# Windowed attention and a gated low-rank layer on one core: the first ten and last eight slots written out as sequences, a new order between them, key/value buffers for each tile

## The chip, the core and the metric

The kernel runs on one core of a Trainium2 chip. A core has five engines with a queue of instructions each: TensorE (PE, matrix products; its weight loads, PEld, run beside them), VectorE (DVE), ScalarE (ACT), GpSimd (POOL) and SyncE (SP, which here only starts DMA transfers). Each engine takes its own instructions in order; between engines there are only semaphores. Products land in PSUM, a small memory in banks of 512 fp32 values for each of 128 partitions; everything else lies in SBUF. The metric is the device time of one execution in microseconds (us), the median of several runs.

## The reference

For each of 32 sequences of 512 tokens with 256 features, all in fp32:

```python
x = x + attn(layernorm(x))     # 16 query heads, 4 key/value heads, head size 64
x = x + ffn(layernorm(x))

# attn: q, k, v = x @ wq.T, x @ wk.T, x @ wv.T;  q, k = rmsnorm(q), rmsnorm(k)
mask = (i >= j) & (i - j < 128)
scores = where(mask, q @ k.T / sqrt(64), -inf)
y = softmax(scores) @ v        # then y @ wo.T

# ffn: gate = softmax(x @ gate_w.T)            (8 experts)
#      out  = x @ weight.T + (1/16) * sum over e of gate[e] * lora_V[e] @ (lora_U[e] @ x)
```

## The kernel before

**Tiles.** A tile is 128 tokens, four to a sequence, 128 in all; `i` counts the tiles and `t = i % 4` is the place in the sequence. A query sees 128 keys, so a tile needs its own keys and values and those of the tile before; at `t == 0` there is no tile before, and a few steps are shorter or fall away (`vdiff`, `pick`, the products with `other`).

**Steps of a tile.** They are methods of `Tile`:
- `ln1_stats`, `ln1_rs` (DVE, POOL): the layernorm's rows. The mean is taken out of the weights instead, by `center` (L194), once for each weight at the start.
- `xT_pe`, `xT_copy`: x is transposed on PE and copied to SBUF by ACT. `kv_pe` and `q_pe(0)`, `q_pe(1)` are the projections.
- Three instructions read the key/value bank: `ksq` (ACT, squares of k), `vdiff` (DVE, two instructions on 64 partitions each: own values minus those of the tile before) and `kv_copy` (ACT, L296). The copy goes into one part of a tile `s.kv` that a sequence shares.
- `q_copy`, `qsq` (ACT), `ksum`, `qsum` (DVE), `pow` (POOL, L214), `kn`, `qn` (POOL): the rmsnorm of q and k.
- `trk`, `trq` (DVE) transpose in blocks of 32, and `move(n)` (L236) carries the blocks across partitions with 16 DMAs from SP's queue. One move takes the probabilities of tile n and the q and k of tile n + 3 together. `kT_copy` (ACT) scales the moved k.
- `s_pe(j)`, j = 0 to 3: the scores of 32 queries; `s_merge`, `nmaxs` (DVE), `exps` (ACT, four exponentials with their sums); `prob_den` (DVE), `prob` (POOL), `tr(j)` (DVE, into the blocks of the move).
- `pick` (POOL), `y_pe`, `y_copy`, `o_pe`, `o_add`: values, output projection, residual.
- `ln2_stats`, `ln2_rs`, `hT_pe`, `hT_copy`, `f_pe`, `gmax`, `gexp`, `gmul`, `uT_pe`, `uT_copy`, `lora_pe`, `store`: the second layer and the write to memory.

**Order.** The scheduler of the framework is switched off for all five engines inside the main block: each engine executes its instructions in the order in which `slot(i)` (L605) writes them. Slot i mixes steps of eight tiles, i to i - 7, and there are 135 slots; in the first seven and last seven some of the tiles don't exist and their steps fall away. The framework adds the semaphores.

**Buffers.** PSUM is divided by a table (L102): four single banks B0 to B3 and two double ones, S0 and S1. Products of one tag share its bank, so a product waits until the last reader of the previous one is through. `BUFS` gives the number of SBUF buffers of each kind. `load_x(i + 3)` at the end of slot i starts the load of a later tile.

Of the kernel before, what the change touches and what calls it, by code (L numbers as in the profile page):

```python
# [8 lines left out]
F32 = mybir.dt.float32  # L9
I32 = mybir.dt.int32  # L10
AF = mybir.ActivationFunctionType
# [3 lines left out]
P = 128  # L15
D = 256
HD = 64
# [13 lines left out]
def tile_window_attn_lora_ffn(  # L31
# [42 lines left out]
    nc = tc.nc  # L74
    B, T, _ = x.shape
    NT = T // P
    N = B * NT
# [3 lines left out]
    KD = KV * HD  # L81
# [3 lines left out]
    AHEAD = 3  # L85
# [10 lines left out]
    seq = ctx.enter_context(tc.tile_pool(name="seq", bufs=3))  # L96
# [4 lines left out]

    BANK = {}  # L102
    for tag, products in {
        "B0": "xT y0 kv uT",
        "B1": "f",
        "B2": "y1 o hT",
        "B3": "q1 q0",
        "S0": "s2 s0",
        "S1": "s1 s3",
    }.items():  # L110
        BANK.update(dict.fromkeys(products.split(), tag))

    def bank(what, name):
        shape = [P, 2, 512] if BANK[what][0] == "S" else [P, 512]
        return psum.tile(shape, F32, tag=BANK[what], name=f"{what}_ps_{name}")
# [1 line left out]

    BUFS = {
        "ksq": 2,
        "q": 2,  # L120
        "qsq": 2,
        "kn": 2,
        "qn": 2,
# [9 lines left out]
        "other": 3,  # L133
        "tr": 2,
        "pT": 2,
    }

    def buf(what, shape, name):
        return work.tile(shape, F32, tag=what, name=f"{what}_{name}", bufs=BUFS[what])
# [5 lines left out]
    xs = {}  # L145

    def load_x(i):
        if i < N:
            b, t = divmod(i, NT)
            xs[i] = work.tile([P, D], F32, tag="x", name=f"x_{b}_{t}", bufs=XBUFS)  # L150
            nc.sync.dma_start(xs[i], x[b, t * P : (t + 1) * P, :])


    for i in range(AHEAD):
        load_x(i)
# [8 lines left out]
    wf_sb = const.tile([P, ND, UG + D], F32, name="wf_sb")  # L164
# [29 lines left out]
    def center(w, what):  # L194

        n = w.shape[-1]
        mean = bank(what, "mean")
        for c in range(ND):
            nc.tensor.matmul(mean[:, :n], mean_m, w[:, c, :], start=(c == 0), stop=(c == ND - 1))
        for c in range(ND):  # L200
            nc.vector.tensor_tensor(w[:, c, :], w[:, c, :], mean[:, :n], ALU.subtract)

    center(wkv_sb, "kv")
    for gp in range(GP):
        center(wq_sb[:, :, gp * 512 : (gp + 1) * 512], f"q{gp}")
    center(wf_sb, "f")

    minus_half = const.tile([P, NH + KV], F32, name="minus_half")
    nc.vector.memset(minus_half, -0.5)
# [26 lines left out]
    def move(n):  # L236
        if not -DELTA <= n < N:
            return
        lo = 0 if n >= 0 else QO
        hi = PIECE if n + DELTA < N else QO  # L240
        moved[n] = buf("pT", [P, NB, PIECE], str(n))
        for b in range(NB):
            for c in range(NB):
                nc.sync.dma_start(  # L244
                    moved[n][b * BL : (b + 1) * BL, c, lo:hi],
                    blocks[n][c * BL : (c + 1) * BL, b, lo:hi],
                )

    class Tile:
# [41 lines left out]
                )  # L291

        def kv_copy(self):
            if self.t == 0:
                self.s.kv = seq.tile([P, NT, 2 * KD], F32, tag="kv", name=f"kv_{self.b}", bufs=3)
            nc.scalar.activation(self.s.kv[:, self.t, :], self.ps["kv"], AF.Copy, scale=self.ln1.rs)  # L296

        def ksq(self):
            self.k_sq = buf("ksq", [P, KD], self.n)
# [35 lines left out]
        def kn(self):  # L335
            self.k_n = buf("kn", [P, KD], self.n)
            nc.gpsimd.tensor_tensor(
                self.k_n.rearrange("p (g d) -> p g d", d=HD),
                self.s.kv[:, self.t, :KD].rearrange("p (g d) -> p g d", d=HD),
                self.rs[:, NH:].unsqueeze(2).to_broadcast([P, KV, HD]),  # L340
                ALU.mult,
            )
# [121 lines left out]
        def vdiff(self):  # L464

            if self.t == 0:
                return
            self.vd = buf("vd", [P, KD], self.n)
            own, old = self.ps["kv"][:, KD:], self.s.kv[:, self.t - 1, KD:]
            lo, hi = slice(0, H), slice(H, P)  # L470
            nc.vector.scalar_tensor_tensor(  # L471
                self.vd[lo], own[lo], self.ln1.rs[lo], old[lo], ALU.mult, ALU.subtract
            )
            nc.vector.scalar_tensor_tensor(  # L474
                self.vd[hi], own[hi], self.minus_rs[hi], old[hi], ALU.mult, ALU.add
            )

        def y_pe(self):


            ps = [self.bank(f"y{e}") for e in range(2)]

            def product(gp, half, e, v, w, start, stop):
                v0 = (2 * gp + half) * HD
                nc.tensor.matmul(  # L485
                    ps[e][half * HD : (half + 1) * HD, gp * 4 * H : (gp + 1) * 4 * H],
                    v[:, v0 : v0 + HD],
                    w.rearrange("p h (c a q) -> p a h c q", c=2, a=2)[:, half],
                    start=start, stop=stop, skip_group_check=True,
                )  # L490

            for gp in range(GP):
                for e in range(2):
                    v = self.s.kv[:, max(self.t - 1 + e, 0), KD:]
                    for half in range(2):
                        product(gp, half, e, v, self.probs(gp, e), gp == 0, self.t == 0)
            if self.t > 0:
                for gp in range(GP):
                    for half, e in ((0, 0), (1, 1), (1, 0), (0, 1)):
                        rows = slice(e * H, (e + 1) * H)  # L500
                        product(gp, half, e, self.vd[rows], self.other[gp][rows], False, True)
# [92 lines left out]
    tiles = {}  # L594
# [5 lines left out]
    nothing = Nothing()  # L600

    def at(i):
        return tiles[i] if 0 <= i < N else nothing

    def slot(i):  # L605
        if 0 <= i < N:
            tiles[i] = Tile(i)
        at(i).ln1_stats()
        at(i).xT_pe()
        at(i - 7).f_pe()  # L610
        at(i - 4).tr(2)
        at(i).xT_copy()
        at(i - 1).q_copy(0)
        at(i).ln1_rs()
        at(i - 4).tr(3)
        at(i - 1).qsq(0)
        at(i - 6).y_pe()
        at(i - 3).exps(0)
        at(i - 7).ln2_rs()
        at(i - 1).qsum()  # L620
        at(i - 4).tr(0)
        at(i - 1).pow()
        at(i - 4).tr(1)
        at(i - 3).s_pe(2)
        at(i - 6).y_copy(0)
        at(i - 7).gmax()
        at(i - 3).s_pe(1)
        at(i - 6).y_copy(1)
        at(i - 3).s_merge(2)
        at(i).kv_pe()  # L630
        at(i - 7).gexp()
        at(i - 3).nmaxs(2)
        at(i - 3).s_merge(1)
        at(i - 3).nmaxs(1)
        at(i - 7).gmul()
        at(i - 6).o_pe()
        at(i).ksq()
        at(i).vdiff()
        at(i - 1).kn()
        at(i).kv_copy()  # L640
        at(i - 1).qn()
        at(i - 2).kT_copy()
        at(i).ksum()
        at(i - 3).exps(2)
        at(i - 1).trk()
        at(i - 5).pick(0)
        at(i - 3).exps(1)
        at(i - 1).trq()
        at(i - 7).uT_pe()
        at(i).q_pe(1)  # L650
        at(i - 3).prob_den(1)
        at(i - 6).o_add()
        at(i - 7).uT_copy()
        move(i - 4)
        at(i - 3).prob(1)
        at(i - 3).prob_den(0)
        at(i - 6).ln2_stats()
        at(i - 2).s_pe(3)
        at(i).q_copy(1)
        at(i - 2).s_pe(0)  # L660
        at(i).qsq(1)
        at(i - 2).s_merge(3)
        at(i - 6).hT_pe()
        at(i - 2).nmaxs(3)
        at(i - 3).prob(0)
        at(i - 7).lora_pe()
        at(i).q_pe(0)
        at(i - 6).hT_copy()
        at(i - 2).s_merge(0)
        at(i - 2).nmaxs(0)  # L670
        at(i - 2).exps(3)
        at(i - 7).store()
        at(i - 5).pick(1)
        load_x(i + AHEAD)

    with tc.manual_schedule(engines={mybir.EngineType.PE, mybir.EngineType.Activation, mybir.EngineType.DVE, mybir.EngineType.Pool, mybir.EngineType.SP}):
        for i in range(N + 7):
            slot(i)

# [1 line left out]
_INS = ["x", "wq", "wkv", "wo", "norm_w", "w_ug", "w_base", "w_v"]  # L681
# [45 lines left out]
```

## Time and profile before

| | |
|---|---|
| median of 3 runs (lowest to highest) | 2259.92 us (2259.31 to 2261.94) |
| the profiled execution | 2258.15 us |
| its span, first to last instruction | 2256.2 us |
| mean granted TensorE clock | 0.989 |
| DMA | 257.77 MB, mean 114 GB/s |
| q1 (all but the loads of constants), share of 16 engines | 46.5% |

All durations below are from the one profiled execution. A row of the table of groups has the line, the engine, the operation, the tile written and those read, then the count, the busy time in us and the mean in ns. A row of the timeline has the start in us, the length, and the same names; what stands in brackets is idle time of the engine before it and who ended it. A row of the table of waits has who waited for whom, the sum in us, how often, and the longest. Matmuls overlap, so the time that one takes is read from start to start, not from its length. Every fp32 matmul appears as two instructions.

### The profile page before, as it was taken

The numbers are of one execution on the slowest core, as the hardware profiler recorded it, in microseconds if no ns is written. First come the engines' busy times: TensorE is split into PE (matmuls) and PEld (weight loads), VectorE is DVE, ScalarE is ACT, GpSimd is POOL, SyncE is SP. The second block draws the span as 40 slices with busy tenths as digits, with TensorE's granted clock in tenths as the row PEclk, the third lists the DMA queues.
The fourth block names the chain that finished last, engine by engine and source line by source line (L and its number), as shares of the span: only waits on it lengthen the run. The fifth ranks groups of instructions, "written<-read, shape, count | busy, mean of one in ns | idle before, by whom it ended". The sixth has DMA issues, their size and how long they took to land.

```text
span 2256.2 us, 43995 instructions
## 1 busy us (share of the span) xinstructions
PE 2145.9 (95%) x12688; PEld 1340.5 (59%) x12688; DVE 1734.7 (77%) x4300; ACT 1508.3 (67%) x5889; POOL 1807.1 (80%) x1771
## 2 busy tenths in 40 slices
PE   5799999999999999999999999999999999999997
PEld 2366566666566666566666566666566666566654
DVE  3577877777877777877777877777877777877773
ACT  2567667767767767767767767767767767767762
POOL 3598788888888888888888888888888888888873
PEclk8799999999999999999999999999999999999999
DMA  2344444544544454544544544544544544544542
GB/s 93 72 111 116 119 118 114 120 118 114 120 118 114 118 120 114 123 116 114 122 117 113 123 116 114 123 116 113 123 116 114 123 116 113 123 116 114 123 112 65
DMA packets 140127, 257.77 MB, mean 114 GB/s; under 512 B 37872, under 2 KB 73840, under 8 KB 139888
## 3 DMA queue, kind: packets, MB, share of 16 engines
q1 hardware_dynamic: 137472, 251.81, 46.5%
q10 hardware_dynamic: 2416, 3.16, 0.4%
q8 instruction: 103, 1.69, 0.3%
q14 instruction: 136, 1.11, 0.2%
HBM read 19.93 MB, written 16.78 MB: 16 GB/s over the span
## 4 chain that ended last, share of the span: by engine, by line
PE 66%; ACT 17%; DVE 9%; issue 4%; SPq 2%; DMA 1%; POOL 1%; ACTq 1%; DVEq 0%; POOLq 0%
PE y_ps L485 14%; PE s_ps L387 13%; PE q_ps L305 12%; ACT ex L414 12%; PE kv_ps L289 8%; PE f_ps L543 7%; PE o_ps L512 5%; PE f_ps L581 2%; ACT kT L369 2%; DVE nmax L403 2%; PE hT_ps L530 2%; DVE vd L474 2%; DVE vd L471 2%; SPq L244 2%; PE xT_ps L277 1%
## 5 line engine op out<-in xcount | busy, mean ns | idle before, releaser
L414 ACT ACTIVATE ex<-s_ps,nmax 128x128 f32<-128x128 f32 x2048 | 722.1, 381 | 13.2 <-DVE nmax L403 11.7
L426 POOL TENSOR_TENSOR ex<-ex,rden 128x1024 f32<-128x1024 f32 x256 | 479.9, 1896 | 130.9 <-DVE rden L422 125.8
L305 PE MATMUL q_ps<-wq_sb,xT 128*128 128x512 f32 x1024 | 489.0, 600 | 3.2 <-ACT qsq L318 3.2
L512 PE MATMUL o_ps<-wo_sb,yT 128*128 128x256 f32 x2048 | 463.5, 379 | 3.7 <-ACT yT L506 3.7
L214 POOL TENSOR_TENSOR rs<-rs,minus_half 128x20 f32<-128x20 f32 x128 | 457.5, 3574 | 10.7
L512 PEld LDWEIGHTS o_ps<-wo_sb,yT 128*128 128x128 f32 x2048 | 388.6, 190 | 110.2 <-issue 58.4
L414 ACT ACTIVATION_READ_ACCUMULATOR ex<-s_ps,nmax 128x1 f32 x2048 | 454.0, 222 | 0.0
L387 PEld LDWEIGHTS s_ps<-kT,pT 64*128 64x128 f32 x4000 | 276.5, 187 | 194.6 <-ACT ex L414 135.6
L387 PE MATMUL s_ps<-kT,pT 64*128 64x160 f32 (+4 forms) x4000 | 329.7, 300 | 45.9 <-ACT ex L414 45.9
L403 DVE TENSOR_REDUCE nmax<-s_ps 128x4 f32<-128x512 f32 x512 | 353.8, 691 | 17.6
L457 POOL TENSOR_SCALAR_AFFINE_SELECT other<-pT 64x512 f32<-64x512 f32 x384 | 299.9, 781 | 22.2 <-DMA pT<-tr 9.5
L305 PEld LDWEIGHTS q_ps<-wq_sb,xT 128*128 128x128 f32 x1024 | 187.2, 193 | 150.1 <-issue 129.4
L437 DVE STREAM_TRANSPOSE tr<-ex 128x256 f32<-128x256 f32 (+3 forms) x512 | 239.7, 487 | 29.1 <-DMA pT<-tr 25.0
L289 PE MATMUL kv_ps<-wkv_sb,xT 128*128 128x512 f32 x512 | 257.8, 626 | 1.0 <-ACT xT L283 1.0
L485 PE MATMUL y_ps<-pT,kv 128*64 128x256 f32 x2048 | 250.1, 386 | 0.5 <-ACT xT L283 0.5
L506 ACT COPY yT<-y_ps 128x512 f32<-128x512 f32 x256 | 138.6, 599 | 160.6 <-PE y_ps L485 160.6
L346 POOL TENSOR_TENSOR qn<-q,rs 128x1024 f32<-128x1024 f32 x128 | 243.4, 1901 | 0.0
L398 DVE COPY_PREDICATED s_ps<-over,s_ps 128x128 f32<-128x128 int32 x512 | 149.5, 292 | 98.9 <-PE s_ps L387 94.4
L300 ACT ACTIVATE ksq<-kv_ps,ln_rs_a 128x256 f32<-128x256 f32 x128 | 60.6, 473 | 243.3 <-PE kv_ps L289 232.3
L485 PEld LDWEIGHTS y_ps<-pT,kv 128*64 128x64 f32 x2048 | 136.1, 137 | 128.0 <-ACT q L313 50.8
L543 PE MATMUL f_ps<-wf_sb,hT 128*128 128x392 f32 x512 | 193.2, 500 | 18.0 <-ACT xT L283 12.1
L313 ACT ACTIVATE q<-q_ps,ln_rs_a 128x512 f32<-128x512 f32 x256 | 182.7, 714 | 27.9 <-PE q_ps L305 27.9
(83 smaller groups left out, 2716.3 us busy)
## 6 DMA issues: line engine op xcount, KB each, us to landing
pT<-tr SPq DMA_DIRECT2D x2000, 104.0 KB, 2.2
x<-in_x_dram SPq DMA_DIRECT2D x128, 128.0 KB, 2.3
out_dram<-res SPq DMA_DIRECT2D x128, 128.0 KB, 1.9
pT<-tr SPq DMA_DIRECT2D x48, 64.0 KB, 2.0
wq_sb<-in_wq_dram ACTq DMA_DIRECT2D x1, 1024.0 KB, 7.1
wo_sb<-in_wo_dram ACTq DMA_DIRECT2D x1, 1024.0 KB, 9.3
pT_-3_205<-tr_-3_199 SPq DMA_DIRECT2D x16, 40.0 KB, 1.9
pT_-2_274<-tr_-2_268 SPq DMA_DIRECT2D x16, 40.0 KB, 1.9
```

Source lines behind the costliest of these rows:

```text
L214: nc.gpsimd.tensor_tensor(o, o, minus_half[:, :n], ALU.pow)
L289: nc.tensor.matmul(ps, self.xT[:, c, :], wkv_sb[:, c, :], start=(c == 0), stop=(c == ND - 1))
L305: nc.tensor.matmul(ps, self.xT[:, c, :], wq_sb[:, c, gp * 512 : (gp + 1) * 512], start=(c == 0), stop=(c == ND - 1),)
L346: nc.gpsimd.tensor_tensor(self.q_n.rearrange("p (g d) -> p g d", d=HD), self.q.rearrange("p g (h d) -> p (g h) d", d=HD), self.rs[:, :NH]. ...
L387: nc.tensor.matmul(ps[:, half, gp, o0:n], qT[rows, gp * P : (gp + 1) * P], self.s.kT[rows, gp, k0 + o0 : k0 + n], start=True, stop=True,)
L403: nc.vector.tensor_reduce(self.nmax[j], ps[:, :, :, :P], AX.X, ALU.max, negate=True)
L414: nc.scalar.activation(self.ex[e][:, c, gp, half], ps[:, gp, half, :P], AF.Exp, bias=self.nmax[j][:, gp, half : half + 1], accum_out=self. ...
L426: nc.gpsimd.tensor_tensor(ex, ex, self.rden[e].rearrange("p c g a -> p (c g a)").unsqueeze(2).to_broadcast([P, 8, P]), ALU.mult,)
L457: nc.gpsimd.affine_select(out=self.other[gp][rows].rearrange("p h (c a q) -> p h c a q", c=2, a=2), in_=fr.rearrange("p h (c a q) -> p h c ...
L485: nc.tensor.matmul(ps[e][half * HD : (half + 1) * HD, gp * 4 * H : (gp + 1) * 4 * H], v[:, v0 : v0 + HD], w.rearrange("p h (c a q) -> p a ...
L512: nc.tensor.matmul(ps[:, :D], self.yT[:, c].rearrange("p e t -> p (e t)"), wo_sb[:, c, :], start=(c == 0), stop=(c == NCH - 1),)
L543: nc.tensor.matmul(ps[:, : UG + D], self.hT[:, c, :], wf_sb[:, c, :], start=(c == 0), stop=(c == ND - 1),)
```

## The change

Four things are changed; no operation is added or removed, and each tile goes through the same steps.

1. The first ten slots become one list, `FIRST`, and the last eight another, `LAST`. An entry is an operation, an argument and a tile (`s_pe.2:0` is `s_pe(2)` of tile 0; in `LAST`, tiles count from the end). `in_order` calls them one by one. `slot(i)` runs for i = 10 to 127 only.
2. Within `slot` the order is new. All four `s_pe` of tile i - 3 are in slot i (before, two of them were in the slot before); `uT_copy`, `lora_pe` and `store` belong to tile i - 8 instead of i - 7, `hT_pe` to i - 7 instead of i - 6, `pick(1)` to i - 6 instead of i - 5. The products are divided anew among the PSUM banks.
3. `kv_copy` writes a buffer of its own for each tile (eight of them) instead of a part of the sequence's tile; `kn`, `vdiff` and `y_pe` read there. q has three buffers instead of two.
4. The centring of the weight `wf` moves from the start into `FIRST`, behind `q_pe.0:2`.

```diff
-        "B0": "xT y0 kv uT",
-        "B1": "f",
-        "B2": "y1 o hT",
-        "B3": "q1 q0",
-        "S0": "s2 s0",
-        "S1": "s1 s3",
+        "B0": "xT hT y0 kv",
+        "B1": "q1 uT",
+        "B2": "y1 o q0",
+        "B3": "f",
+        "S0": "s0 s2",
+        "S1": "s3 s1",
...
-        "q": 2,
+        "q": 3,
...
+        "kv": 8,
...
-        if i < N:
+        if i < N and i not in xs:
...
-    center(wf_sb, "f")
...
         def kv_copy(self):
-            if self.t == 0:
-                self.s.kv = seq.tile([P, NT, 2 * KD], F32, tag="kv", name=f"kv_{self.b}", bufs=3)
-            nc.scalar.activation(self.s.kv[:, self.t, :], self.ps["kv"], AF.Copy, scale=self.ln1.rs)
+            self.kv = buf("kv", [P, 2 * KD], self.n)
+            nc.scalar.activation(self.kv, self.ps["kv"], AF.Copy, scale=self.ln1.rs)
...
-            own, old = self.ps["kv"][:, KD:], self.s.kv[:, self.t - 1, KD:]
+            own, old = self.ps["kv"][:, KD:], tiles[self.i - 1].kv[:, KD:]
```

The order of a slot after the change, and the two lists cut to their beginnings and ends (one line of the slot holds several calls here; `-3` is tile i - 3):

```
ln1_stats:0 xT_pe:0 s_pe.0:-3 uT_copy:-8 tr.2:-4 xT_copy:0 s_pe.3:-3 ln1_rs:0 q_copy.0:-1
s_merge.0:-3 qsq.0:-1 hT_pe:-7 nmaxs.0:-3 q_pe.1:0 pick.1:-6 hT_copy:-7 qsum:-1 exps.0:-3
s_merge.3:-3 lora_pe:-8 nmaxs.3:-3 pow:-1 q_copy.1:0 y_pe:-6 tr.3:-4 qsq.1:0 tr.0:-4 exps.3:-3
tr.1:-4 store:-8 s_pe.2:-3 y_copy.0:-6 s_pe.1:-3 y_copy.1:-6 kn:-1 s_merge.2:-3 f_pe:-7 qn:-1
kT_copy:-2 trk:-1 nmaxs.2:-3 o_pe:-6 s_merge.1:-3 nmaxs.1:-3 exps.2:-3 pick.0:-5 trq:-1 exps.1:-3
prob_den.1:-3 gmax:-7 move:-4 prob.1:-3 gexp:-7 kv_pe:0 prob_den.0:-3 o_add:-6 ln2_stats:-6
prob.0:-3 gmul:-7 q_pe.0:0 ksq:0 vdiff:0 kv_copy:0 ln2_rs:-6 ksum:0 uT_pe:-7 load_x:+3
```
```diff
+    FIRST = """
+        ln1_stats:0 xT_pe:0 ln1_stats:1 xT_copy:0 ln1_rs:0 q_pe.1:0 ln1_stats:2 ln1_stats:3 ln1_rs:1
+        kv_pe:0 q_copy.1:0 ln1_rs:2 qsq.1:0 q_pe.0:0 ln1_rs:3 vdiff:0 ksq:0 kv_copy:0 ksum:0 xT_pe:1
+        q_copy.0:0 xT_copy:1 qsq.0:0 q_pe.1:1 qsum:0 kv_pe:1 pow:0 q_copy.1:1 qsq.1:1 q_pe.0:1
+        vdiff:1 ksq:1 kv_copy:1 ksum:1 xT_pe:2 q_copy.0:1 kn:0 xT_copy:2 qsq.0:1 qn:0 q_pe.1:2 trk:0
+        qsum:1 kv_pe:2 pow:1 trq:0 q_copy.1:2 qsq.1:2 move:-3 q_pe.0:2 center_f:0 vdiff:2 ksq:2
...
+        xT_pe:4 q_copy.0:3 kn:2 xT_copy:4 qsq.0:3 qn:2 q_pe.1:4 qsum:3 move:-2 kv_pe:4 ln1_rs:4
+        pow:3 trk:2 kT_copy:0 trq:2 q_copy.1:4 s_pe.0:0 qsq.1:4 s_pe.3:0 ksq:4 s_merge.0:0 kv_copy:4
...
+    LAST = """
...
+        nmaxs.3:-3 tr.3:-4 exps.3:-3 s_pe.2:-3 tr.0:-4 store:-8 y_copy.0:-6 s_merge.2:-3 kn:-1
+        s_pe.1:-3 nmaxs.2:-3 y_copy.1:-6 qn:-1 f_pe:-7 trk:-1 s_merge.1:-3 nmaxs.1:-3 kT_copy:-2
+        o_pe:-6 pick.0:-5 exps.1:-3 trq:-1 gmax:-7 pick.1:-5 move:-4 prob_den.0:-3 gexp:-7 exps.2:-3
...
+        store:-3 ln2_rs:-2 y_pe:-1 f_pe:-2 y_copy.0:-1 y_copy.1:-1 o_pe:-1 gmax:-2 gexp:-2 gmul:-2
+        uT_pe:-2 o_add:-1 uT_copy:-2 ln2_stats:-1 hT_pe:-1 lora_pe:-2 hT_copy:-1 ln2_rs:-1 store:-2
+        f_pe:-1 gmax:-1 gexp:-1 gmul:-1 uT_pe:-1 uT_copy:-1 lora_pe:-1 store:-1
+    """
+
+    def in_order(table, base):
+        for entry in table.split():
+            op, i = entry.split(":")
+            op, _, arg = op.partition(".")
+            i = base + int(i)
+            if op == "center_f":
+                center(wf_sb, "f")
+                continue
+            if op == "move":
+                move(i)
+                continue
+            if i not in tiles:
+                load_x(i + AHEAD)
+            getattr(at(i), op)(*map(int, arg))
+
     with tc.manual_schedule(engines={...}):
-        for i in range(N + 7):
+        in_order(FIRST, 0)
+        for i in range(10, N - 1 + 1):
             slot(i)
+        in_order(LAST, N)
```

## The prediction

> **What bounds the kernel now.** I read the page first (busy shares and slices), then the table of waits, then one period of TensorE (PE) in order of time, then the reads of one key/value bank, then both ends of the run.
>
> ```profile
> PE 2145.9 (95%) x12688; PEld 1340.5 (59%) x12688; DVE 1734.7 (77%) x4300; ACT 1508.3 (67%) x5889; POOL 1807.1 (80%) x1771
> PE   5799999999999999999999999999999999999997
> PEclk8799999999999999999999999999999999999999
> ```
> PE is the bound from the third slice to the last; nothing else is above 80%. The slack is in the first two slices (113 us), the last one, and in small waits between. The waits:
>
> ```profile
> ACT kv L296 <- DVE vd L474: 115.7, 96, 1.7
> PE s_ps L387 <- ACT ex L414: 61.0, 101, 3.8
> DVE vd L471 <- ACT ksq L300: 31.8, 65, 3.3
> ```
> Only the second is PE's own. The steady run repeats every four tiles (one sequence): xT starts at 1004.78 and again at 1072.47, so 67.69 us for four slots, 16.92 each. One slot of these has no wait on PE:
>
> ```profile
> 1022.78 0.38 PE L277 MATMUL xT_ps<-ident,x 128*128 128x128 f32 x2
> 1028.60 1.98 PE L289 MATMUL kv_ps<-wkv_sb,xT 128*128 128x512 f32 x4
> 1030.42 3.62 PE L512 MATMUL o_ps<-wo_sb,yT 128*128 128x256 f32 x16
> 1033.98 1.88 PE L305 MATMUL q_ps<-wq_sb,xT 128*128 128x512 f32 x4
> ...
> 1039.51 0.38 PE L277 MATMUL xT_ps<-ident,x 128*128 128x128 f32 x2
> ```
> First column start, second length. 1022.78 to 1039.51 is 16.73 us: the floor of a full slot. Start to start, that is xT 0.22, f 1.41, y 1.88+1.02, s 1.29 twice, kv 1.82, o 3.45, uT 0.11, q 1.81+1.72, hT 0.27, lora 0.43. In the other three slots q to s takes 2.63, 2.15 and 2.14 instead of 1.81 (s waits for the exponentials of its bank), and xT to f once 0.79 instead of 0.22: 0.82+0.34+0.33+0.57, and 0.07 three times for the restart, 2.27 us in 67.69. The floor of four slots is 65.42, 16.36 each.
>
> **The change, the middle (118 slots, tiles 10 to 127).** All matmuls stay. Switches between full and 64-row tiles cost about 0.1 each (q to s 1.81 against q to xT 1.72), and there are six in both orders, so the floor stays. I laid the new order out against this floor, xT at 0: s0 and s3 0.3 to 1.6, hT, q1 1.9, lora 3.6, y 4.1, s2 and s1 7.0 to 8.3, f 8.3, o 9.7, kv 13.2, q0 14.9, uT 16.6, next xT 16.73.
>
> The waits of s go. exps of s0 end near 3.8 and of s3 near 6.4 (1.36 per call, with q_copy and qsq, 0.58 each, between); s2 and s1 need their banks at 7.0 and 7.7. exps of s2 and s1 end near 10.4 and 11.8, needed at 17. With a short y (first tile of a sequence) s1 comes at 6.7 and still fits. f needs the store of the tile before (VectorE, DVE, near 6.8, needed 8.3). GpSimd (POOL) has 15.6 us of work in a full slot (pow 3.9, two prob 3.8, picks 3.2, qn and kn 2.5, the rows of two layernorms 2.2), less than a slot. SyncE's 16 move DMAs take 10.1 us; trq ends near 11.3, they land 2 us after the last, near 6 of the next slot, before kT_copy near 8. The transposes of DVE keep their order behind them. That is worth up to 2.27 per four slots, 67 us in 118 slots.
>
> What is late next is the key/value bank. It has three readers on two engines, and xT shares it (B0 in both orders):
>
> ```profile
> 1045.33 1.98 PE L289 MATMUL kv_ps<-wkv_sb,xT 128*128 128x512 f32 x4
> 1047.41 0.47 ACT L300 ACTIVATE ksq<-kv_ps,ln_rs_a 128x256 f32<-128x256 f32 x1 [1.89 <-PE kv_ps L289]
> 1047.91 0.48 DVE L471 SCALAR_TENSOR_TENSOR vd<-kv_ps,ln_rs_a,kv 64x256 f32<-64x256 f32 x1 [0.54 <-ACT ksq L300]
> 1048.40 0.49 DVE L474 SCALAR_TENSOR_TENSOR vd<-kv_ps,minus_rs,kv 64x256 f32<-64x256 f32 x1
> 1048.93 0.69 ACT L296 ACTIVATE kv<-kv_ps,ln_rs_a 128x512 f32<-128x512 f32 x1 [1.05 <-DVE vd L474]
> ```
> They read one after the other: 4.29 us from the first kv matmul to the end of the last read, 4.19 without the switch from s. Before, o (3.45), uT and q1 lie behind kv and hide it. Now only q0 (1.72) and uT (0.11) do: xT can start at 13.18 + 4.19 + 0.06 (an exponential's end to its s: 1018.94 to 1019.00) = 17.43 instead of 16.73. **A new wait of 0.70 us**, in the three slots of four that have a vdiff; without vdiff the copy ends near 16.3 and nothing waits. PE is in order, so the whole next slot queues behind this xT.
>
> Do the own buffers remove kv_copy's wait for vdiff? Read by the row alone, kv_copy could wait because it writes the tile of which vdiff reads the previous part; then the wait falls and the stall is 0. But vdiff waits for ksq with no tensor between them except the bank (it starts 0.03 after ksq ends). The Trainium skill, PSUM — Partial Sum Buffer, "PSUM bank collisions raise a hardware error", says that two engines must not be in one bank and the same 32 partitions at once, reads against reads included. By that rule own buffers change nothing: middle (65.42 + 3 x 0.70)/4 = 16.88. By the buffer reading 16.36. I take the rule: 118 x (16.92 - 16.88) = **5 us saved** (0 to 10; the 0.06 and the switch penalties are good to 0.1 us per slot, so -7 to +17). Third q buffer, eight kv buffers: no reader of a buffer is still at work when its turn comes (y of tile i-7 reads kv of i-8 a slot before it is overwritten): nothing. Loads of x come earlier in FIRST, 0.45 each on an SP that is idle until 30: nothing.
>
> **The first ten slots.** Before, slot 10 starts at 176.34. Its PE work at floor rates (ten xT, kv, q; seven s; four y and o; three f) is 102 us. Why so long:
>
> ```profile
> 26.35 3.56 POOL L214 TENSOR_TENSOR rs<-rs,minus_half 128x20 f32<-128x20 f32 x1
> 33.76 10.09 SPq L244 DMA_DIRECT2D pT_-3_205<-tr_-3_199  x16
> 45.83 1.99 PE L387 MATMUL s_ps<-kT,pT_-3_205 64*128 64x128 f32 x16 [10.36 <-ACT kT L369]
> ```
> The scores of tile 0 wait for pow, the transposes and a 10 us move, and PE has nothing else in its order. FIRST gives it five tiles of projections there. The q of tile 0 starts near 14.7 (without f's centring, 1.3, and with q0 and q1 in two banks, 1.2 idle before). Each tile takes 5.4 of PE, 0.8 for the read chain and 0.5 for xT to its copy to q: 6.7. Centring f moves behind q0 of tile 2: its two subtracts (0.5 each) stand on DVE before vdiff of tile 2 and wait for 1.4 us of matmuls, so xT of tile 3 comes some 4 us later; in all it costs more than the 1.3 it saves at the head. s of tile 0 near 49. Next is the ladder of moves: SP issues one per 10.7 us, and the third also waits for the last s of tile 0 (its buffer), so s of tile 2 is near 68. Between 52 and 68 PE has about 5 us of work: 11 idle. At 52, 74 us are left; from 68 on y and o are there and PE leads (13 to 16 us per move against 10.7; POOL's chain ends near 140). 52 + 11 + 74 = 137, 3 for waits as in the middle.
>
> The clock comes on top: the slices show 0.8, 0.7, and by 20 us windows it was 0.59, 0.70, 0.74 between 40 and 100, with PE 56 to 71% busy. The row applied to the 18 us of work after the gap costs 8 (18/0.7 - 18). The skill, TensorE: Matmul & The Clock Gate, Part 1, says that the clock halves after about 3.4 us of idling and is back after as much sustained work: three such gaps x 3.4 x 1/2 = 5. I take 6: **slot 10 at 146, 30 saved** (20 to 40).
>
> **The last eight.** Before, slot 128 starts at 2173.58 and the span ends 82.6 later; left for PE are 59 us.
>
> ```profile
> 2219.23 10.01 SPq L244 DMA_DIRECT2D pT<-tr  x16
> 2238.48 1.95 PE L485 MATMUL y_ps<-pT,kv 128*64 128x256 f32 x16
> ```
> The last move has landed near 2231 but its y waits for its slot until 2238. LAST has 61 us of PE work (s3 and s0 moved in, 2 us). The last tile's chain: pow and qn to 8.5, trq 9.7, move to 19.8, s near 22.5, exponentials to 32; three more moves back to back, the last issued 40 to 50, landed 52; picks to 55; y held by PE's own backlog to 55. Before, y to the end took 17.7: **73 instead of 82.6, 10 saved** (4 to 14).
>
> **Sum.** 5 + 30 + 10 = 45: the profiled span 2256.2 becomes 2211, its execution (2258.15) 2213, and the shown median stands 1.8 above that one: **2215**.
>
> **Rivals.** (a) The own buffers do free kv_copy, or its wait hides: the middle runs at 16.36, 118 x 0.56 = 66 instead of 5: 2154. For it: the three-reader chain would be visible in the code's own pipeline; against it: vdiff's wait for ksq. (b) Slower: vdiff is later than ksq. On DVE it stands behind o_add, ln2_stats and gmul, which start only when o ends (13.4) and end near 15.1, 0.5 before ksq does. If DVE runs more than that late (77% busy, and it waits for qn in trq), every further us is one us of xT in 88 slots. The ends' 45 is eaten when DVE is 1.0 us late; at 1.3 late it is 0.8 x 88 = 70 more: 2285. Against it: the replay leaves DVE idle from 12.2 to 13.4. (c) The fill's gaps stay (POOL's 6.5 us per tile and the ladder set the pace) and the drain is held by picks: 12 and 5 instead of 30 and 10: 2238. That the order isn't executed as written has nothing for it: PE's rows above follow the slot line by line.
>
> **Numbers.** Forecast 0.70 (own range 2196 to 2236), (a) 0.08, (b) 0.10, (c) 0.12. Range 2172 to 2248: it takes in (c) and leaves out (a) and (b). About 0.2% (4.5 us) can be told from no change: faster 0.87, same 0.03, slower 0.10.
>
> **What would show it.** xT waiting for the ACT copy of kv, 0.7 us, three times in four slots, and s hardly waiting for ex: right. No wait at xT and 65.4 per four slots: (a). vd starting more than 0.1 after ksq ends: (b). Slot 10's xT later than 160: the fill is wrong. The last y more than 60 after slot 128 starts: the drain is wrong.

## The result and the profile after

The changed kernel takes 2220.17 us (median of 5 runs, 2218.7 to 2221.07) against 2259.92 before: ratio 0.983, 95% interval 0.982 to 0.984. The forecast was 2215, its range 2172 to 2248. The profiled execution took 2220.7 us, with a span of 2219.0 at a mean clock of 0.993. The page of the changed kernel, its busy times and two rows of its slices:

```profile
PE 2140.9 (96%) x12688; PEld 1343.6 (61%) x12688; DVE 1718.5 (77%) x4300; ACT 1529.3 (69%) x5889; POOL 1806.2 (81%) x1771
PE   7799999999999999999999999999999999999998
PEclk9799999999999999999999999999999999999999
```

The first two slices are fuller than before (7 and 7 against 5 and 7), the last one too. The span lost 37.2 us. It is cut here in three: at the xT of slot 10, and at PE's first product of slot 128 (f at 2173.58 before, s at 2144.34 after):

| part | before, us | after, us | saved | forecast |
|---|---|---|---|---|
| start to slot 10 | 176.34 | 151.84 | 24.5 | 30 |
| slots 10 to 127 | 1997.24 | 1992.50 | 4.7 | 5 |
| slot 128 to the end | 82.6 | 74.7 | 8.0 | 10 |

In the steady run four slots take 67.58 us from xT to xT (before 67.69). The table of waits of the changed kernel (who waited for whom: sum in us, times, longest) shows what they hold now:

```profile
PEld xT_ps L277 <- ACT kv L295: 100.0, 94, 3.8
ACT kv L295 <- DVE vd L473: 93.4, 89, 1.1
DVE vd L470 <- ACT ksq L299: 59.4, 90, 0.7
...
PE s_ps L386 <- ACT ex L413: 4.9, 6, 2.1
...
PE xT_ps L277 <- ACT kv L295: 33.8, 64, 3.2
PE xT_ps L277 <- DMA pT<-tr: 13.8, 29, 0.5
```

PE's wait of s for the exponentials fell from 61.0 us in 101 places to 4.9 in 6. In its stead the transpose of x waits for the key/value copy, 94 times; the copy for vdiff, vdiff for ksq. The first row is that of the weight loads. PE's own idle time before xT stands in the last two rows: in 29 places the profile names a DMA instead, which xT doesn't read. The timeline of the changed kernel shows one such chain (start, length, idle time before in brackets):

```profile
1042.50 1.88 PE L289 MATMUL kv_ps<-wkv_sb,xT 128*128 128x512 f32 x4
...
1044.42 0.47 ACT L299 ACTIVATE ksq<-kv_ps,ln_rs_a 128x256 f32<-128x256 f32 x1 [1.74 <-PE kv_ps L289]
1044.92 0.47 DVE L470 SCALAR_TENSOR_TENSOR vd<-kv_ps,ln_rs_a,kv 64x256 f32<-64x256 f32 x1 [0.69 <-ACT ksq L299]
1045.41 0.49 DVE L473 SCALAR_TENSOR_TENSOR vd<-kv_ps,minus_rs,kv 64x256 f32<-64x256 f32 x1
1045.93 0.27 PE L573 MATMUL uT_ps<-ident,u 128*128 128x128 f32 x1
1045.94 0.69 ACT L295 ACTIVATE kv<-kv_ps,ln_rs_a 128x512 f32<-128x512 f32 x1 [1.05 <-DVE vd L473]
...
1046.68 0.44 PE L277 MATMUL xT_ps<-ident,x 128*128 128x128 f32 x2 [0.47 <-ACT kv L295]
```

Each reader begins 0.02 to 0.04 us after the one before it ends. From the first kv matmul to the end of the copy it is 4.13 us, and xT starts 0.05 later. It comes 0.75 us after uT, start to start; in run 11 below, where it waits for nothing, it comes 0.11 after it.

The opening of the changed kernel on PE:

```profile
32.12 1.48 PE L200 MATMUL f_ps_mean<-wf_sb,mean_m 128*128 128x392 f32 x4
36.77 0.44 PE L277 MATMUL xT_ps<-ident,x 128*128 128x128 f32 x2 [3.17 <-ACT kv L295]
...
49.81 1.16 PE L386 MATMUL s_ps<-kT,pT_-3_253 64*128 64x32 f32 x16
...
60.80 2.57 PE L386 MATMUL s_ps<-kT,pT_-2_348 64*128 64x160 f32 x16 [4.69 <-ACT kT L368]
65.49 2.91 PE L386 MATMUL s_ps<-kT,pT_-2_348 64*128 64x160 f32 x16 [2.11 <-ACT ex L413]
...
71.57 2.57 PE L386 MATMUL s_ps<-kT,pT_-1_451 64*128 64x160 f32 x16 [2.56 <-ACT kT L368]
```

The moved centring (first row) is followed by 3.17 us of idle PE, and from 52.9 to 71.6 PE stands for 10.95 us in all. At the end, the last y starts 56.5 us after slot 128:

```profile
2200.87 1.95 PE L484 MATMUL y_ps<-pT,kv 128*64 128x256 f32 x16
```

### The profile page after: what moved, and what is told of

It is laid out like the page before. It is cut to its first block, busy times and chain, and to the rows that moved or that the text cites. A ratio compares the mean times of both kernels' runs of the same rounds, so it can differ in the third digit from the quotient of the medians.

```text
span 2219.0 us, 44224 instructions
## 1 busy us (share of the span) xinstructions
PE 2140.9 (96%) x12688; PEld 1343.6 (61%) x12688; DVE 1718.5 (77%) x4300; ACT 1529.3 (69%) x5889; POOL 1806.2 (81%) x1771
## 4 chain that ended last, share of the span: by engine, by line
PE 77%; DVE 8%; SPq 5%; ACT 4%; DMA 3%; issue 2%; POOL 1%; ACTq 0%; DVEq 0%; POOLq 0%
PE o_ps L511 15%; PE y_ps L484 15%; PE s_ps L386 13%; PE q_ps L304 13%; PE kv_ps L289 8%; PE f_ps L542 7%; SPq L244 5%; DMA pT<-tr 3%; PE f_ps L580 2%; DVE nmax L402 2%; PE hT_ps L529 2%; PE xT_ps L277 2%; ACT kv L295 2%; DVE tr L360 2%; DVE vd L473 1%
## 5 line engine op out<-in xcount | busy, mean ns | idle before, releaser
L413 ACT ACTIVATION_READ_ACCUMULATOR ex<-s_ps,nmax 128x1 f32 x2048 | 441.5, 216 | 0.0
L402 DVE TENSOR_REDUCE nmax<-s_ps 128x4 f32<-128x512 f32 x512 | 348.8, 682 | 13.3
L386 PEld LDWEIGHTS s_ps<-kT,pT 64*128 64x128 f32 x4000 | 271.4, 186 | 75.1 <-issue 63.3
L289 PE MATMUL kv_ps<-wkv_sb,xT 128*128 128x512 f32 x512 | 241.5, 594 | 0.0
L542 PE MATMUL f_ps<-wf_sb,hT 128*128 128x392 f32 x512 | 202.7, 518 | 0.7 <-DVE res L587 0.7
L312 ACT ACTIVATE q<-q_ps,ln_rs_a 128x512 f32<-128x512 f32 x256 | 177.2, 692 | 15.3 <-PE q_ps L304 14.0
L317 ACT ACTIVATE qsq<-q_ps,ln_rs_a 128x512 f32<-128x512 f32 x256 | 176.6, 690 | 0.0
```

The lines of the kernel that those rows point to most:

```text
L289: nc.tensor.matmul(ps, self.xT[:, c, :], wkv_sb[:, c, :], start=(c == 0), stop=(c == ND - 1))
L386: nc.tensor.matmul(ps[:, half, gp, o0:n], qT[rows, gp * P : (gp + 1) * P], self.s.kT[rows, gp, k0 + o0 : k0 + n], start=True, stop=True,)
L402: nc.vector.tensor_reduce(self.nmax[j], ps[:, :, :, :P], AX.X, ALU.max, negate=True)
L413: nc.scalar.activation(self.ex[e][:, c, gp, half], ps[:, gp, half, :P], AF.Exp, bias=self.nmax[j][:, gp, half : half + 1], accum_out=self. ...
L542: nc.tensor.matmul(ps[:, : UG + D], self.hT[:, c, :], wf_sb[:, c, :], start=(c == 0), stop=(c == ND - 1),)
```

## The experiments

Eleven kernels were run. Where an edit of the slot is shown, the two lists were fitted to it. A ratio is to the kernel before, with its 95% interval. "Four slots" is the steady time of one sequence, xT to xT, which is 67.58 in the changed kernel and 65.42 at the floor that the prediction worked out.

### 1 and 2. vdiff taken out of the bank

Theory: the wait at xT is the bank's chain of three readers. In the changed kernel vdiff was made to read the SBUF copies, behind `kv_copy`; the same edit was made in the kernel before.

```diff
-        at(i).vdiff()
         at(i).kv_copy()
+        at(i).vdiff()
...
-            nc.vector.scalar_tensor_tensor(self.vd[lo], own[lo], self.ln1.rs[lo], old[lo], ALU.mult, ALU.subtract)
-            nc.vector.scalar_tensor_tensor(self.vd[hi], own[hi], self.minus_rs[hi], old[hi], ALU.mult, ALU.add)
+            nc.vector.tensor_tensor(self.vd[lo], own[lo], old[lo], ALU.subtract)   # own: the SBUF copy
+            nc.vector.tensor_tensor(self.vd[hi], old[hi], own[hi], ALU.subtract)
```

> The kernel after the change; vdiff subtracts the two SBUF copies of v (after kv_copy) instead of reading the key/value bank, so the bank has two readers, both on ACT. Theory (three serial reads of the bank hold back the next xT by 0.70 us in three slots of four): the chain from the first kv matmul to the last read falls from 4.19 to about 3.1 us, xT hardly waits, four slots take 65.4 to 66.0 us instead of 67.56, total 2171 (2162 to 2185). Some 0.5 us per four slots may come back as s waiting for ex, since vdiff now ends later on DVE. Rival (the wait at xT has another cause, or DVE gives it back): 2212 or more.

> The same edit in the kernel before the change, where o, uT and q1 stand between kv and the next xT. Theory: the waits of s for ex there (2.27 us per four slots) are the same chain in another place, since kv_copy holds up the exponentials behind it on ACT; with the copy 1 us earlier most of them fall: four slots 65.5 to 66.5 instead of 67.69, total 2200 (2190 to 2225). Rival (o hides the chain there, and the waits of s are a matter of the order of the scores alone): 2255 to 2262.

Measured: changed kernel so edited 2231.47, ratio 0.988 (0.986 to 0.989), four slots 67.93: a miss, slower than without the edit. The waits of this kernel, and three rows of its timeline, the last of them in the slot behind the first two:

```profile
DVE vd L470 <- ACT kv L295: 110.2, 94, 3.0
PE s_ps L386 <- ACT ex L413: 59.6, 96, 2.3
```

```profile
1034.78 0.42 DVE L470 TENSOR_TENSOR vd<-kv,kv 64x256 f32<-64x256 f32 x1 [1.26 <-ACT kv L295]
1035.21 0.42 DVE L471 TENSOR_TENSOR vd<-kv,kv 64x256 f32<-64x256 f32 x1
...
1042.67 0.81 PE L386 MATMUL s_ps<-kT,pT 64*128 64x160 f32 x8 [0.55 <-ACT ex L413]
```

The wait at xT is gone as the theory says (xT follows uT by 0.11), but s waits for the exponentials again, nearly as long as in the kernel before. vdiff now stands on VectorE until `kv_copy` has ended, and behind it in VectorE's order stand ksum, the transposes, merges and maxima that the exponentials need. PE starts its slot 0.7 us earlier and VectorE ends vdiff later. A second effect lies on top: the same 64x256 subtraction takes from 0.38 to 2.03 us. Run 5 shows why. In the rows above both subtractions take 0.42, and s waits 0.55 all the same, so that wait doesn't need the slowed subtractions.

The kernel before so edited: 2238.55, ratio 0.991 (0.990 to 0.993), four slots 67.22, between the theory and its rival. PE's wait of s for the exponentials fell from 61.0 us to 26.1, as the theory says, but a new wait took most of that place:

```profile
PE f_ps L539 <- DVE res L584: 40.2, 36, 1.3
```

This is f waiting for VectorE's part of the store. Of the 20 us that this edit saved there, 8.5 lie ahead of slot 10 (176.34 to 167.83).

### 3. The old buffers

The changed kernel with the sequence's shared key/value tile and two buffers of q.

```diff
-        "q": 3,
+        "q": 2,
...
-        "kv": 8,
...
-            self.kv = buf("kv", [P, 2 * KD], self.n)
+            if self.t == 0:
+                self.s.kv = seq.tile([P, NT, 2 * KD], F32, tag="kv", name=f"kv_{self.b}", bufs=3)
+            self.kv = self.s.kv[:, self.t, :]
```

> The kernel after the change with the buffers of before: kv_copy writes a part of the sequence's tile again, and q has two buffers. Theory (kv_copy waits for vdiff because of the bank, not because of the tile; no buffer is waited for): no change, 2216 to 2225. Rival (the own buffers carry part of the gain): 2228 or more, with new waits of ACT kv or of q.

Measured 2222.18, ratio 0.984 (0.983 to 0.986), four slots 67.60 against 67.58. The own buffers are worth nothing that this shows; the chain is that of the bank.

### 4. The new slot order alone

`slot(i)` for all 136 slots, without the two lists, `wf` centred at the start.

```diff
-        in_order(FIRST, 0)
-        for i in range(10, N - 1 + 1):
+        for i in range(N + 8):
             slot(i)
-        in_order(LAST, N)
```

> The new slot order alone: 136 slots, no FIRST and no LAST, f centred at the start. Theory (the gain is in the two ends, the middle gives 5 us): the middle stays at 67.56 per four slots and the ends go back, 2220 + 24.5 + 8 = 2252 (2240 to 2262). Rival (the new slot order carries the gain and the lists little): 2220 to 2232.

Measured 2239.93, ratio 0.992 (0.990 to 0.993): a miss of 12 us. Slot 10 starts at 157.57, so 18.8 of the 24.5 us at the head come with the slot order and not with the list. In this kernel the scores of tile 0 come right behind the fourth xT, while the kernel before stood 10.36 us for them in the slot before, with that projection still to come:

```profile
45.37 0.44 PE L278 MATMUL xT_ps<-ident,x 128*128 128x128 f32 x2 [3.84 <-ACT kv L296]
```

They start 0.37 us behind it, at 45.74. At the end the order alone does worse: from the last tile's xT to the end 104.28 us, against 100.61 before and 91.06 with `LAST`.

### 5 and 6. vdiff one slot later, and with it the edits of 7 and 10

Theory: with vdiff of tile i - 1 in slot i, VectorE no longer stands for `kv_copy`. It was put where VectorE was idle, ahead of `o_add`. The second kernel adds the later centring and the earlier key copies of the runs below.

```diff
         at(i - 3).prob_den(0)
+        at(i - 1).vdiff()
         at(i - 6).o_add()
...
-        at(i).vdiff()
```

> As e1_vd_from_sbuf, but vdiff of tile i - 1 stands in slot i ahead of o_add, where DVE waited for o_pe (0.97 us in the kernel after the change), instead of directly behind kv_copy. Theory (in e1 the wait at xT was gone, but vdiff held up ln1_stats and the first nmaxs of the next slot, so exps came late and s1 waited): with vdiff out of the way neither xT nor s waits, four slots take 65.4 to 66.2 us instead of 67.58, total 2165 (2156 to 2180). Rival (s waits for ex again by more than 1 us per four slots, because the floor of 65.4 is not in reach with POOL at 15.6 us per slot): 2190 or more.

> e8 and e7 together, and in FIRST kT_copy of tiles 1 and 2 ahead of exps that stood before it on ACT (tile 1's move had landed near 53 and its copy began at 60.2). Theory: 3 to 6 us less than e8, total 2161 (2150 to 2176). Rival (POOL or the moves set the pace of the fill): as e8.

Measured 2448.62, ratio 1.084 (1.083 to 1.086), and 2448.47, ratio 1.084 (1.083 to 1.086): a large miss, both alike, four slots 75.15. The timeline of the first (a POOL row with x2 is two instructions in a row):

```profile
1009.28 3.93 POOL L425 TENSOR_TENSOR ex<-ex,rden 128x1024 f32<-128x1024 f32 x2 [0.51 <-DVE lg L545]
...
1009.65 1.80 DVE L470 TENSOR_TENSOR vd<-kv,kv 64x256 f32<-64x256 f32 x1
...
1011.47 2.03 DVE L471 TENSOR_TENSOR vd<-kv,kv 64x256 f32<-64x256 f32 x1
...
1013.53 0.42 DVE L514 TENSOR_TENSOR h<-o_ps,x 128x256 f32<-128x256 f32 x1
...
1014.01 3.57 PE L304 MATMUL q_ps<-wq_sb,xT 128*128 128x512 f32 x4 [2.65 <-DVE h L514]
```

GpSimd divides the probabilities in two instructions of 1.96 us, and each subtraction beside one of them ends only after it: the second POOL instruction ends at 1013.21, the second subtraction at 1013.50. Of all 192 subtractions, 180 begin while such a division runs, and the median of them ends 0.28 us after the GpSimd instruction. That makes 3.83 us where 0.84 was due; `o_add` comes 3 us late, and q0, which needs its bank, lets PE stand: 2.65 us here, 184.6 us in 90 places in all. The clock adds to it: the q0 shown takes 3.57 us instead of 1.88, at a granted clock of 0.54 from 1014.01 to 1017.37, and the mean clock of the execution fell from 0.993 to 0.958. The form that reads PSUM isn't touched: in the changed kernel it lay beside the same divisions and took 0.475 to 0.493. The Trainium skill, SBUF — State Buffer, "SBUF: two separate sides", has the rule: a VectorE operation with two SBUF inputs and a GpSimd operation that reads SBUF share a pair of ports, and who starts first holds it for the whole instruction. I had looked for idle time of VectorE and not for what runs on GpSimd beside it.

### 7 and 8. The centring of wf, later and at the start

```diff
-  q_pe.0:2 center_f:0 vdiff:2
+  q_pe.0:2 vdiff:2
...
-  qn:3 s_pe.2:0
+  qn:3 center_f:0 s_pe.2:0
```

The other kernel drops the entry and centres `wf` at the start, as before.

> The kernel after the change with the centring of f in FIRST moved from behind q0 of tile 2 to ahead of s2 of tile 0, where PE idles. Theory (centring holds up vdiff of tile 2 and with it xT of tile 3 by some 4 us, and the scores of tile 0 and the third move follow): xT of tile 3 near 33, slot 10 starts 2 to 4 us earlier, total 2217 (2215 to 2220). Rival (the ladder of moves or POOL sets the pace behind it): slot 10 within 1 us of 151.8, 2219 to 2222.

> The kernel after the change with f centred at the start again, as before the change. Theory (the move costs more than the 1.3 us of PE that it takes from the head): xT of tile 3 about 2.5 us earlier, slot 10 1 to 3 us earlier, total 2218 (2216 to 2221). Rival (the move saves what it takes from the head): 2221 to 2224.

Measured: later 2215.98, ratio 0.981 (0.979 to 0.982); at the start 2216.70, ratio 0.981 (0.980 to 0.982). Slot 10 starts at 146.31 and 147.32 instead of 151.84. Both beat the changed kernel, by 4.2 and 3.5 us of the medians: the place of the centring costs more than it saves. Most of it is clock, as windows cut where the granted clock changes show (length; busy time and count of PE, PEld, DVE, ACT, POOL; granted clock; DMA share; GB/s). Up to slot 10 the clock is 1.00 outside these windows in both kernels. The changed kernel:

```profile
38.62:42.03 3.41, 3.41 (x5) 1.33 (x4) 2.48 (x4) 1.26 (x2) 2.40 (x2) 0.50 0.32 96
55.68:76.16 20.48, 11.12 (x58) 8.14 (x57) 15.37 (x37) 11.53 (x59) 9.54 (x9) 0.50 0.36 87
86.40:89.82 3.42, 3.42 (x6) 1.17 (x4) 3.15 (x7) 1.56 (x9) 3.33 (x4) 0.50 0.49 110
```

With the later centring:

```profile
55.41:72.48 17.07, 11.09 (x53) 8.02 (x54) 13.86 (x34) 8.90 (x45) 8.80 (x9) 0.50 0.42 102
```

As an estimate, half of PE's busy time in these windows is what the clock cost: 1.7 + 5.6 + 1.7 make 9.0 us in the changed kernel, 5.5 with the later centring. The 3.5 between them is most of the 5.5 at slot 10. The wait at xT of tile 3 fell from 3.17 to 0.50, and PE's idle time up to slot 10 is 3.2 us less in all. The two add up to more than the 5.5, so the estimate of the clock is good to about 1 us.

### 9. The key copies earlier

In the changed kernel `kT_copy` of tile 1 stands on ScalarE behind exponentials until 60.2. To the later centring was added:

```diff
-  exps.3:0 qn:3
+  exps.3:0 kT_copy:1 qn:3
...
-  exps.2:1 s_merge.1:1
+  exps.2:1 kT_copy:2 s_merge.1:1
```

> The changed kernel with the centring of the base weight moved behind the first projections of the fifth tile (as in the run that did this alone, 2216.0), and the key copies of tiles 1 and 2 put ahead of one group of exponentials on ScalarE in the opening. Theory (the second tile's scores start at 60.8 and the third's at 71.6 because the key copies stand behind exponentials on ScalarE, not because their moves land late): each start comes 1 to 3 us earlier and 1 to 3 us less at the head, 2214 (2212 to 2216). Rival (the moves, whose 16 issues take 10 us each on the queue, set those starts): 2216 to 2217, no gain beside the centring's.

Measured 2217.10, ratio 0.982 (0.981 to 0.984): no gain beside the centring's, the rival holds. With the later centring alone the scores of tile 1 had started at 56.50 already. The timeline of this kernel:

```profile
54.05 0.51 ACT L368 ACTIVATE kT<-pT_-2_343,key_w 128x256 f32<-128x256 f32 x1 [3.76 <-DMA pT_-1_452<-tr_-1_369]
...
56.58 2.90 PE L386 MATMUL s_ps<-kT,pT_-2_343 64*128 64x160 f32 x16 [5.51 <-ACT ex L413]
```

ScalarE now stands 3.76 us for the move, and the exponentials of tile 0 that free the banks queue behind it. The copy is early and the scores are not.

### 10. ksq taken out of the bank

On the kernel of run 9, ksq reads the SBUF copy, so the bank has two readers in a row.

```diff
-        at(i).ksq()
         at(i).vdiff()
         at(i).kv_copy()
+        at(i).ksq()
...
-            nc.scalar.activation(self.k_sq, self.ps["kv"][:, :KD], AF.Square, scale=self.ln1.rs)
+            nc.scalar.activation(self.k_sq, self.kv[:, :KD], AF.Square)
```

> The kernel of the run before, and the key squares read the key/value tile from SBUF after its copy instead of the bank ahead of it, so the bank has two readers in a row (value difference 0.96, copy 0.69) in place of three. Theory (the 0.70 us at the transpose of x, in three slots of four, is the sum of the bank's serial readers): one reader of 0.47 and its handover leave the chain, the wait falls from 0.70 to some 0.2 and four slots from 67.58 to some 66.1, 29.5 groups of four give 44 us, 2171 (2162 to 2185). Rival (another wait takes the place at once, as it did when the value difference left the bank): four slots stay above 67.2 and the time above 2200.

Measured 2236.15, ratio 0.991 (0.989 to 0.993), four slots 68.15: the rival. Its timeline:

```profile
1047.37 0.47 DVE L470 SCALAR_TENSOR_TENSOR vd<-kv_ps,ln_rs_a,kv 64x256 f32<-64x256 f32 x1 [0.18 <-PE kv_ps L289]
1047.86 0.49 DVE L473 SCALAR_TENSOR_TENSOR vd<-kv_ps,minus_rs,kv 64x256 f32<-64x256 f32 x1
1048.44 0.69 ACT L295 ACTIVATE kv<-kv_ps,ln_rs_a 128x512 f32<-128x512 f32 x1 [2.61 <-DVE vd L473]
...
1049.18 0.44 PE L277 MATMUL xT_ps<-ident,x 128*128 128x128 f32 x2
...
1049.61 0.42 DVE L321 TENSOR_REDUCE ss<-ksq 128x4 f32<-128x256 f32 x1 [1.26 <-ACT ksq L299]
...
1057.36 0.66 PE L386 MATMUL s_ps<-kT,pT 64*128 64x64 f32 x8 [0.61 <-ACT ex L413]
```

xT does follow sooner, 0.30 after uT instead of 0.75. But ksum (the row of L321), in VectorE's order ahead of all that the next exponentials need, stands 1.26 us for ksq, and s waits 0.61. What was gained at xT is paid at s, as in run 1: PE's slot begins earlier and VectorE's doesn't.

### 11. vdiff beside the power operation

Run 5 with another place: right behind the store's VectorE operation, where VectorE is idle for 1.4 us and GpSimd works at `pow`, 128x20. In the opening vdiff reads the bank as before. The base is the kernel of run 9.

```diff
         at(i - 8).store()
+        at(i - 1).vdiff()
...
-        at(i).vdiff()
...
+            if self.i >= 9:
+                own = self.kv[:, KD:]
+                nc.vector.tensor_tensor(self.vd[lo], own[lo], old[lo], ALU.subtract)
+                nc.vector.tensor_tensor(self.vd[hi], old[hi], own[hi], ALU.subtract)
+                return
```

> The kernel of the first run of this call, and from tile 9 on the value difference of the tile before is taken from the SBUF copies, right after the store's last VectorE operation, while GpSimd works at the small power operation (128x20, 3.57 us) and VectorE is idle for 1.4 us. In the opening it reads the bank as before. Theory (the loss in the two runs with the difference read from SBUF came only from VectorE standing until a wide two-input GpSimd operation beside it had ended): the two subtractions take 0.42 us each, the wait at the transpose of x goes and no other comes, four slots take 65.4 to 66.2, 2158 (2148 to 2175). Rival (reading from SBUF is slow beside any GpSimd operation, or VectorE's order is what cost): four slots stay above 67.2 and the time above 2200.

Measured **2154.9** (2153.78 to 2155.5), ratio 0.955 (0.953 to 0.956): 65 us less than the changed kernel by the medians, four slots 65.46. Its page and its timeline:

```profile
PE 2117.5 (98%) x12688; PEld 1346.3 (63%) x12688; DVE 1700.5 (79%) x4300; ACT 1525.3 (71%) x5889; POOL 1803.2 (84%) x1771
```

```profile
1011.64 0.47 ACT L299 ACTIVATE ksq<-kv_ps,ln_rs_a 128x256 f32<-128x256 f32 x1 [1.76 <-PE kv_ps L289]
1012.01 0.68 ACT L295 ACTIVATE kv<-kv_ps,ln_rs_a 128x512 f32<-128x512 f32 x1
...
1013.15 0.27 PE L579 MATMUL uT_ps<-ident,u 128*128 128x128 f32 x1
...
1013.26 0.38 PE L277 MATMUL xT_ps<-ident,x 128*128 128x128 f32 x2
...
1017.60 3.56 POOL L214 TENSOR_TENSOR rs<-rs,minus_half 128x20 f32<-128x20 f32 x1
...
1020.52 0.40 DVE L472 TENSOR_TENSOR vd<-kv,kv 64x256 f32<-64x256 f32 x1
1020.94 0.42 DVE L473 TENSOR_TENSOR vd<-kv,kv 64x256 f32<-64x256 f32 x1
```

The bank is free 0.46 us before uT, xT waits for nothing, and all 180 of these subtractions start while `pow` runs, 2.0 to 3.4 us after it began, and take 0.40 to 0.42 us. The same instructions in run 5 took 1.5 and 2.0 (medians), so it was the neighbour that made them slow. Of the text on record one word is too strong: in run 1 the loss came not only from that neighbour but also from VectorE's standing for the copy. In run 1 s waited 0.55 us in a slot whose two subtractions were not slowed. This run removes both causes. Giving xT another bank than kv, the other way to be rid of the wait, was not tried.

## Why the prediction was right, and what was mis-sized

**The middle** came as worked out: 16.88 per slot forecast, 67.58/4 = 16.89 measured. The waits of s went, and the 0.70 at xT took their place. Run 3 shows that the own buffers carry none of it, run 11 that the chain of readers is all of it: without vdiff in the bank and with nothing else made late, four slots take 65.46, and the floor on record was 65.42. Slot by slot, over one sequence, the changed kernel lies 0.06, 0.63, 0.70 and 0.70 us above run 11; the forecast had nothing and three times 0.70. That is rival (a)'s middle by another road; the buffers alone don't bring it. Rival (b), vdiff later than ksq, did not happen: vd starts 0.02 to 0.03 after ksq ends.

**The first ten slots**: right in kind, 24.5 instead of 30. The scores of tile 0 start at 49.8 (forecast near 49); the idle time is 10.95 (11), from 52.9 instead of 52. From there to slot 10 it takes 88.0 us without that idle time; the forecast had 74 of work, 3 of waits and 6 of clock, 83. The waits are 3.0. By the windows at runs 7 and 8 the half clock behind 52.9 cost 7.3, 1.3 more than the 6. The other 3.7 is work: as an estimate, good to about 1 us as the clock's is, 77.7 at full clock. So the term that was mis-sized most is "At 52, 74 us are left": it took the products at their rates in the steady run. Which of them take longer in the opening, and why, was not looked into.

Of the clock's term the reasoning is off too. It counted three gaps at 3.4 us of half clock each, or the 18 us of work after them. In the trace the clock stays at 0.50 for 20.48 us without a break, through the gaps and the work between them (PE is busy 11.12 of it), and for 3.42 us once more. The 3.17 us that the centring opens ahead of them is a fourth gap: behind it lie 3.41 us at 0.50, in which the q and kv matmuls took 2.88 and 2.73 for 1.98 and 1.88. That 1.7 lies ahead of 52.9. With this gap gone (run 7) slot 10 starts at 146.31. That this is the forecast's 146 is chance: the forecast had the centring's 4 us in it. The scores of tile 2 started at 71.6, not 68, without moving the sum.

**The centring.** That its new place "costs more than the 1.3 it saves" holds: 3.5 us against the old place. The forecast put 4 us at xT of tile 3; it was 2.7 of wait (3.17 against 0.50 in run 7) and 1.7 of slower matmuls behind it, 4.4.

**Where the head's gain lies** was told wrongly: not mostly in `FIRST`. The slot order alone brings 18.8. The list brings 10.3 more with the centring at the start (157.57 to 147.32), and its centring gives 4.5 back.

**The last eight**: 74.7 instead of 73, the last y 56.5 after slot 128 instead of 55. So 1.5 of the 1.7 lie ahead of that y, in the backlog. Against the new order's own end `LAST` is worth 13.2 (run 4): the new order would have lost 3.7 there.

**Rivals**: (c), small gains at both ends, is out. The total is 5 us above the forecast by the medians: 5.5 less saved at the head, 2 at the end and 0.3 in the middle, less 2.6 because the forecast set the median 3.8 above the span and it came out 1.2 above it.

## What to carry to other kernels

Where several engines read one PSUM bank, add up their readers in a row and hold the sum against the work that the next user of the bank has ahead of it. To shorten such a chain, take a reader away only if its new place makes nothing late in the in-order queue it stands in: three of the four ways tried here moved the wait instead of removing it. Before placing a two-input SBUF operation on VectorE, look at what GpSimd runs at that moment, not only for idle time on VectorE.

## What the hardware showed beyond that

VectorE's 64x256 subtraction with both inputs in SBUF waits for the end of a wide GpSimd operation beside it: the division (128x1024) in run 5, qn in run 2, where the median subtraction beside qn took 1.56 us and ended 0.28 us after it, and pick (64x512, one input) in run 2, where 60 subtractions took a median 0.88 us and ended 0.26 after it. Beside `pow`, which is also a two-input GpSimd operation and runs for 3.56 us, but on 128x20, it took 0.40 to 0.42 us in 180 of 180 cases in run 11, and 0.42 in four cases in run 2 that begin 0.3 to 0.8 us after it. The rule cited at run 5 would hold the ports for that whole instruction too; the measurement says no. Why, no run here shows.

The clock's price depends on more than the idle time. Runs 9 and 11 have the same opening up to tile 9. Between 48 and 76 us PE stood 11.55 us in run 9 and 12.07 in run 11, and yet run 9 had the half clock longer. Run 9, then run 11:

```profile
53.29:73.77 20.48, 11.55 (x53) 8.10 (x54) 13.18 (x32) 11.63 (x58) 8.76 (x8) 0.50 0.33 79
```

```profile
53.44:67.09 13.65, 6.42 (x34) 4.72 (x34) 7.98 (x19) 8.20 (x40) 3.75 (x2) 0.50 0.18 47
67.09:70.50 3.41, 1.81 (x17) 1.40 (x18) 2.39 (x7) 2.69 (x14) 2.37 (x3) 1.00 0.65 151
70.50:73.92 3.42, 3.42 (x5) 1.35 (x6) 3.42 (x11) 1.33 (x8) 3.16 (x5) 0.50 0.68 161
```

Slot 10 starts at 147.69 and 146.61: about 1 us between two executions of one opening, so a difference of that size at the head, such as that between runs 7 and 8, says nothing. Every stretch of half clock shown in these openings is 3.41 us or a multiple of it, and within one execution all changes lie on one grid of that step (38.62, 42.03, 55.68, 76.16, 86.40, 89.82 in the changed kernel). The skill, TensorE: Matmul & The Clock Gate, Part 1, has the clock decided in windows that run on their own and don't start with a gap, so the same idle time can cost more or less by where it falls; these rows agree with it.
